# PSUM operands, GpSimd minima and a shorter backward scan in the WKV ratio of a fused two-layer kernel

## The chip, the cores and the metric

The kernel runs on one core of one Trainium2 chip, as one launch. The metric is the device time of the whole program in microseconds. A core has five engines that each run their own instruction queue: PE (TensorE, matmuls), DVE (VectorE), ACT (ScalarE), POOL (GpSimd) and SP (SyncE, which here issues the DMAs). On-chip memory is SBUF (128 partitions) and PSUM (128 partitions, here used as banks of 128x512 float32; matmuls write to it). All data is float32.

## The reference

Four sequences of 256 tokens with 256 channels pass two layers. Each layer is: condition the activations, mix the tokens, add; condition again, a feed-forward net with experts, add. In layer 0 the mixing is a gated delta-rule attention, and the net has 64 experts; in layer 1 the mixing is a gated linear block, and the net has 8 experts. What the change touches above all is the conditioner, which occurs four times, with its own `w` and `u` (k and v are both the side input f, r is the activation):

```python
def _bi_wkv(r, k, v, w, u, time_emb):
    tf = sigmoid(sum(time_emb, axis=-1))[:, None, None]
    decay = exp(-exp(w))[None, :] * (0.5 + 0.5 * tf[:, :, 0])
    ek = exp(minimum(kf, 30.0))
    ekv = ek * vf
    # step: a = a * decay + ekv_t ; b = b * decay + ek_t, kept after every token
    _, (nf, df) = scan(step, 0, (ekv_t, ek_t))
    _, (nb, db) = scan(step, 0, (ekv_t, ek_t), reverse=True)
    euk = exp(minimum(u + kf, 30.0))
    num = nf + nb - ekv + euk * vf
    den = df + db - ek + euk
    base = sigmoid(r) * (num / maximum(den, 1e-08))
    return base * (0.8 + 0.2 * tf)
```

Everything but `sigmoid(r)` depends on the inputs alone, so `num / den` (the ratio) of all four conditioners can be made at any time before it is needed.

The attention of layer 0, per head and chunk of 64 tokens:

```python
g = cumsum(-exp(a_log) * softplus(x @ w_a + dt_bias))       # log decay in the chunk
q, k, v = split(silu(conv4(x @ w_qkv)))                     # q and k are then l2-normed
A = where(strict, -(beta * k @ k.T) * exp(g_i - g_j), 0)
attn = solve_triangular(I - A, I)                           # a 64x64 unit triangular inverse
v_c, k_c = attn @ (v * beta), attn @ (k * beta * exp(g))
# then a scan over the chunks with a 128x128 state per head
out = rmsnorm(o) * norm_w * silu(x @ w_z) @ w_out
```

## The kernel before

**Tape and plan.** The program isn't issued as it is written. Every piece of work is recorded with `Tape.op` (line 195): its engine, an assumed cost in us, the function that emits its instructions, the buffers it reads and writes, and, for ACT, the function table that it needs. [...] `pushed` (391) works new latest starts out of a finished plan, and `run` (405) plans again with them, up to `ROUNDS` times. Of these plans it takes the one with the lowest end (`min(plans)`, line 413), and emits all operations in the order of their starts. Each engine keeps the emitted order (`Ordered`, 118). So the instruction order of every engine, and the order in which buffers go round, come out of the plan, and any changed cost or constant (lines 421 to 428) may change the order anywhere in the program. All recorded instructions carry line 128 in the profile; they are told apart by the names of their tiles.

**Buffers.** `ps` (1474) hands out six PSUM banks that all uses share: convolutions (`ps_cvq`, `ps_cvk`, `ps_cvv`), Gram matrices (`ps_gram`), norms (`ps_kt`), 32- and 64-wide products of the inverse (`ps_at` and others, `ps_lu`), `ps_z`, `ps_wo`, the experts (`ps_h`, `ps_a`, `ps_e`, `ps_ae`). `place` (1464) hands out 59 SBUF tiles of 128x512, and the table `MOST` says how many of these each use may hold at a time.

**Stages.** Tokens go in two halves of 512, s = 0 and 1.

1. Conditioner 0 of half 0 (`conditioned`, `ratio_piece` with c = 0), then `gates` (1679): `ps_gates`, the decay `g` by several small DVE and ACT operations, `ps_decay`, a row form written to DRAM (`G<-rows`), which is read back spread over partitions (`attnT<-G`, per head).
2. Attention in four groups of four key heads per half (`Group`, with a `Unit` per key head that has two value heads). `Unit.products` (882): convolutions with four taps (`convolved`; PE, then three SCALAR_TENSOR_TENSOR on DVE and one ACT activation), Gram matrices, norms (`norms`, `shifted`: squares are summed on PE into a `kt` bank, transposed by DVE into an SBUF tile `turned`, and made into reciprocal norms), the decay masks (`attnT`: DVE or ACT adds, ACT exp, POOL products with `sb_consts`, with `c` and with the Gram matrices `kqm`, which make `X`). `Group.small_inverses` (493): X goes to DRAM (`raw<-X`) and comes back in a layout with one 32x32 problem to a partition (`Rt<-raw`); DVE solves it there by 30 pairs of operations (`prod`, `xs`), transposes it (`Tc`), and DMAs it back through DRAM (`done`). `inverse32` and `inverse64` make the 64x64 inverses with matmuls (`ps_lu` and what follows). Then `values`, `outputs`, `normed`, `project` (`ps_wo`).
3. The 64 experts (`experts64`; weights `w_w` come by DMA for each expert pair), conditioner 2 of layer 1's `gated_mix`, and the 8 experts (`experts8`), each for both halves.

**The ratio** (`ratio_piece`, 1521): a conditioner c has eight pieces, one for each channel half cc and sequence b, each of 128 channels x 256 tokens; 32 in all. The four pieces with c = 0 and s = 0 are "summed": their three terms of `num` and of `den` are added by PE, with an identity matrix, in a PSUM bank. In the other 28, POOL adds them in SBUF, and with c > 0 the result waits in DRAM until its layer needs it. In a piece, DVE makes the two minima, ACT the two exponentials `ek` and `euk`, POOL `ekv`, `euk - ek` and the product with f (into f); DVE makes four scans over 256 tokens (`fwn`, `bwn`, `fwd`, `bwd`), each with the decay of the channel, then the maximum, the reciprocal and the product with the numerator. Both scans include a token itself, which is why `ek` is subtracted once (`num` needs no such operation, as `(euk - ek) * f` has it).

Of the kernel before, what the change touches and what calls it, by code (L numbers as in the profile page):

```python
# [11 lines left out]
AF = mybir.ActivationFunctionType  # L12
ALU = mybir.AluOpType
# [3 lines left out]
P = 128  # L17
# [164 lines left out]
class Tape:  # L182
# [222 lines left out]
    def run(self):  # L405
        latest, plans = self.urgency(), []
        for n in range(ROUNDS):
            last = self.plan(latest)
            if last is None:
                break  # L410
            plans.append((last, n, [(o.start, o.end, o.new) for o in self.ops]))
            latest = self.pushed(last)
        for o, (o.start, o.end, o.new) in zip(self.ops, min(plans)[2]):
            pass
        for o in sorted(self.ops, key=lambda o: (o.start, o.order)):
            for buf in o.new:
                buf()
            o.emit()


ROUNDS, SWITCH, LOAD, SPARE, AHEAD, EACH, END, IDLE, MOMENT, GAP, RATE, GIVES = 10, 14.532, 1.3, 95.787, 163.973, 23.222, 1300.0, 54.829, 0.668, 62.664, 3.14, 4.877
UNIT = 42

EARLY, FEW = range(3, 5), 6
NORMS = 0.55
FOUR32, TWO64 = 0.75, 1.1
LAND = 3.0
WINDOW, ENOUGH, LITTLE, SLOW, THIN = 3.4, 0.471, 0.38, 0.5, 6.598
# [367 lines left out]
class Unit:  # L796
# [85 lines left out]
    def products(self):  # L882
# [65 lines left out]
        turned = self.buf([P, 8, 32], "turned", 2)  # L948
        sums = lambda j: turned().rearrange("p (n j) r -> p n j r", j=2)[:, :, j, 0]
# [28 lines left out]

        op("PE", NORMS, norms, sqs, [ps], to=[turned, k2, ki, self.kn, self.eo])

# [398 lines left out]
class Program:  # L1379
# [82 lines left out]
    MOST = {'attnT': 20, 'kq1': 12, 'kq0': 2, 'kqm': 17, 'cross': 10, 'vo': 18, 'zs': 5, 'oT': 6, 'w0': 5, 'hw0': 9, 'w1': 8, 'hw1': 7, 'wo': 2, 'sq': 4, 'r0': 10, 'wqk': 20, 'vn': 21, 'acck': 22, 'wb0': 3, 'vd': 7, 'U': 5, 'wv': 7, 'qe': 6}  # L1462
# [58 lines left out]
    def ratio_piece(self, c, cc, b):  # L1521
# [28 lines left out]
        op(  # L1550
            "DVE",
            0.45,
            lambda: v.tensor_scalar(
                euk(), f(), self.wu[:, c, 1, cc : cc + 1], 30.0, ALU.add, ALU.min
            ),
# [5 lines left out]
        op("POOL", 0.75, lambda: tt(ekv(), ek(), f(), ALU.mult), [ek, f], [ekv])  # L1561
        op("POOL", 0.75, lambda: tt(euk(), euk(), ek(), ALU.subtract), [ek], [euk])
        op("POOL", 0.75, lambda: tt(f(), euk(), f(), ALU.mult), [euk], [f])
        decay = self.decay[:, c, cc, b : b + 1].to_broadcast([P, T])

        def sums(n, *terms):

            to = ps()[:, n * T : n * T + T]
            for i, x in enumerate(terms):
                last = i == len(terms) - 1  # L1570
                e.tensor.matmul(to, self.const(IDENT), x(), start=i == 0, stop=last)

        def both_ways(src, extra, n):
            fw, bw = new(f"fw{n}"), new(f"bw{n}", f"bw{n}" if summed else "bw")
            op(
                "DVE",
                0.95,
                lambda: v.tensor_tensor_scan(fw(), decay, src(), 0.0, ALU.mult, ALU.add),
                [src, self.decayb],
                [fw],  # L1580
            )
            op(
                "DVE",
                0.95,
                lambda: v.tensor_tensor_scan(
                    bw()[:, ::-1], decay, src()[:, ::-1], 0.0, ALU.mult, ALU.add
                ),
                [src, self.decayb],
                [bw],
            )  # L1590
            if summed:
                i = "nd".index(n)
                op(
                    "PE",
                    _mm(256, 3),
                    lambda: sums(i, fw, bw, extra),
                    [fw, bw, extra],
                    [(ps, {i})],
                )
                return lambda: ps()[:, i * T : i * T + T], (ps, {i})  # L1600
            op("POOL", 0.75, lambda: tt(fw(), fw(), bw(), ALU.add), [bw], [fw])
# [3 lines left out]
        num, numb = both_ways(ekv, f, "n")  # L1605
        sum_, sumb = both_ways(ek, euk, "d")
        den = new("den") if summed else sumb
        op("DVE", 0.45, lambda: v.tensor_scalar_max(den(), sum_(), 1e-8), [sumb], [den], port=True)
        op("DVE", 1.75, lambda: v.reciprocal(den(), den()), [], [den])
# [4 lines left out]
        else:  # L1614
# [7 lines left out]
            [numb, den, self.decayb],  # L1622
            [w],
            port=True,
# [632 lines left out]
```

## Time and profile before

| what | value |
| --- | --- |
| time, median of 3 runs | 1410.57 us (1408.24 to 1412.5) |
| the profiled execution: time, span | 1412.93 us, 1411.1 us |
| mean granted PE clock | 0.982 of full speed |
| PE busy | 1321.2 us, 94% of the span |
| DVE busy | 1064.8 us, 75% |
| POOL busy | 922.8 us, 65% |
| ACT busy | 915.2 us, 65% |
| ACT table loads | 126, 161.7 us |
| chain of waits that ended last, by engine | PE 45%, DVE 25%, ACT 12%, POOL 7%, DMA 6% |
| start of the first 64-wide products (`ps_lu`) of the eight groups | 152, 244, 353, 470, 579, 695, 805, 901 us |

The mean durations of one instruction of a ratio piece (the 26 or 28 that are not among the first), all 128x256:

| engine | instruction | mean ns |
| --- | --- | --- |
| DVE | minimum into `ek`, sum and minimum into `euk` | 491, 562 |
| DVE | scans `fwd`, `bwd`, `fwn`, `bwn` | 913, 837, 881, 1016 |
| DVE | maximum, reciprocal, product with the numerator | 486, 1748, 612 |
| POOL | `ekv`, `euk - ek`, product with f | 730, 823, 782 |
| POOL | the four additions | 728, 956, 767, 748 |

How to read it: "busy" is the time in which an engine worked on an instruction of its own; register and semaphore instructions do not count. A matmul's end is modelled, so a busy PE need not be PE at its peak. The span is one profiled execution from its first to its last instruction; the time of that execution is 1.8 us longer. Where the text below gives a moment, it is a start in us from the start of the span. The engines overlap nearly everywhere, so busy times do not add up to the span.

### The profile page before, as it was taken

Reading aid. Unit: us, or ns where it says so; the run is one execution under the profiler, and the core shown is the slowest. Engines: PE = TensorE matmul, PEld = TensorE weight load, DVE = VectorE, ACT = ScalarE, POOL = GpSimd, SP = SyncE. Lnnn points to the kernel's source line nnn. Section 1 sums busy time; section 2 is a strip of 40 time slices with the busy share of each in tenths; the row PEclk is TensorE's granted clock in tenths of the full one; section 3 lists DMA queues with packets and bytes.
Section 4 is the critical chain, followed back from the end, with each engine's and each line's share of the span. In section 5 each row is a group of like instructions: output and inputs, shape, how many; then the busy total and the mean of one; then the engine's idle time right before and its main releaser. Section 6 shows DMA issues by size and latency. Waiting matters only on the chain.

```text
span 1411.1 us, 24205 instructions
## 1 busy us (share of the span) xinstructions
PE 1321.2 (94%) x8428; PEld 817.4 (58%) x8428; DVE 1064.8 (75%) x2112; ACT 915.2 (65%) x1999; POOL 922.8 (65%) x913
## 2 busy tenths in 40 slices
PE   5986999999999899999999999999999999998988
PEld 3544766765875676766676576555455544443433
DVE  7889798787699588768769879867796787773123
ACT  1797799999889899988898898533434622211220
POOL 3189769979763988976885884487654666762032
PEclk9997999999999999999999999999999999999989
DMA  6412524412322353241351343544532324656030
GB/s 208 129 46 64 128 83 113 125 62 67 91 90 58 71 140 106 50 139 39 94 139 38 76 124 101 150 127 135 153 105 83 103 92 139 181 139 212 0 105 15
DMA packets 149817, 145.39 MB, mean 103 GB/s; under 512 B 76976, under 2 KB 93104, under 8 KB 149696
## 3 DMA queue, kind: packets, MB, share of 16 engines
q1 hardware_dynamic: 149264, 143.45, 35.5%
q8 instruction: 67, 1.10, 0.3%
q14 instruction: 54, 0.44, 0.1%
q10 hardware_dynamic: 432, 0.40, 0.1%
HBM read 129.75 MB, written 14.06 MB: 102 GB/s over the span
## 4 chain that ended last, share of the span: by engine, by line
PE 45%; DVE 25%; ACT 12%; POOL 7%; DMA 6%; issue 5%; SPq 1%; ACTq 0%; POOLq 0%; DVEq 0%
PE ps_h L128 5%; PE ps_a L128 4%; PE ps_ae L128 4%; PE ps_wo L128 4%; PE ps_e L128 4%; PE ps_z L128 4%; DVE xs L128 3%; DVE prod L128 3%; DVE accv_v L128 3%; PE ps_cvv L128 3%; PE ps_at L128 2%; DVE accq_q L128 2%; POOL attnT L128 2%; DMA w_w<-in_w 2%; ACT L128 2%
## 5 line engine op out<-in xcount | busy, mean ns | idle before, releaser
L128 ACT ACT_TABLE_LOAD x126 | 161.7, 1283 | 22.2 <-DVE sb_xT L128 10.4
L128 DVE SCALAR_TENSOR_TENSOR accv_v<-ps_cvv,sb_convw,accv_v 128x510 f32<-128x510 f32 (+2 forms) x192 | 141.8, 744 | 42.3 <-ACT accv_v L128 37.4
L128 PE MATMUL ps_z<-wz,ratio 128*128 128x256 f32 x480 | 118.7, 394 | 9.6 <-DVE vo L128 6.6
L128 POOL TENSOR_TENSOR hw_h<-hw_h,r_h 128x512 f32<-128x512 f32 x64 | 85.7, 1347 | 63.9 <-DVE hw_h L128 63.3
L128 PE MATMUL ps_h<-ratio,w_w 128*128 128x512 f32 x256 | 118.9, 598 | 6.6 <-DMA w_w<-in_w 5.7
L128 PE MATMUL ps_cvv<-ratio,wv 128*128 128x512 f32 x256 | 119.9, 601 | 2.9 <-ACT kqm L128 1.0
L128 ACT ACTIVATE r_h<-ps_h 128x512 f32<-128x512 f32 x64 | 38.2, 596 | 126.8 <-PE ps_h L128 126.5
L128 PE MATMUL ps_a<-hw_h,w_w 128*128 128x512 f32 x256 | 118.2, 593 | 0.0
L128 PE MATMUL ps_wo<-oT,wo 128*128 128x512 f32 x256 | 113.0, 593 | 0.0
L128 POOL TENSOR_TENSOR hw_e<-hw_e,r_e 128x512 f32<-128x512 f32 x32 | 41.6, 1322 | 101.0 <-DVE hw_e L128 101.0
L128 PEld LDWEIGHTS ps_z<-wz,ratio 128*128 128x128 f32 x480 | 90.1, 196 | 24.6 <-DVE vo L128 6.8
L128 PEld LDWEIGHTS ps_h<-ratio,w_w 128*128 128x128 f32 x256 | 47.0, 190 | 70.2 <-issue 55.1
L128 DVE TENSOR_TENSOR xs<-xs,prod 128x30 f32<-128x30 f32 (+14 forms) x240 | 81.2, 338 | 8.2
L128 DVE TENSOR_TENSOR prod<-xs,Rt 128x30 f32<-128x30 f32 (+14 forms) x240 | 78.5, 327 | 11.6 <-ACT xs L128 5.9
L128 ACT ACTIVATE junko<-vo 128x128 f32<-128x128 f32 x256 | 79.3, 310 | 7.6
L128 PE MATMUL ps_at<-vn,attnT 128*128 128x128 f32 x512 | 82.3, 277 | 1.5 <-ACT vn L128 1.4
L128 POOL TENSOR_TENSOR X<-attnT,kqm 128x512 f32<-128x512 f32 x64 | 82.8, 1313 | 1.2 <-ACT kqm L128 1.0
L128 POOL TENSOR_TENSOR vo<-vo,zs 128x512 f32<-128x512 f32 x64 | 81.2, 1288 | 1.6 <-ACT zs L128 1.6
L128 PEld LDWEIGHTS ps_wo<-oT,wo 128*128 128x128 f32 x256 | 48.1, 190 | 57.4 <-issue 52.6
L128 POOL TENSOR_TENSOR attnT<-attnT,sb_consts 128x512 f32<-128x512 f32 x56 | 70.7, 1280 | 15.5 <-DMA attnT<-G 8.5
L128 POOL TENSOR_TENSOR attnT<-attnT,kqm 128x512 f32<-128x512 f32 x64 | 80.6, 1278 | 0.1
L128 PEld LDWEIGHTS ps_a<-hw_h,w_w 128*128 128x128 f32 x256 | 47.9, 190 | 56.2 <-issue 52.6
(253 smaller groups left out, 3412.5 us busy)
## 6 DMA issues: line engine op xcount, KB each, us to landing
attnT<-G SPq DMA_DIRECT2D x64, 256.0 KB, 5.2
w_w<-in_w SPq DMA_DIRECT2D x64, 256.0 KB, 4.4
wb_wb<-w_rows SPq DMA_DIRECT2D x128, 128.0 KB, 3.6
wqk<-in_wqk SPq DMA_DIRECT2D x32, 256.0 KB, 4.2
wv<-in_wv SPq DMA_DIRECT2D x32, 256.0 KB, 4.2
wo<-in_wo SPq DMA_DIRECT2D x32, 256.0 KB, 3.8
qe<-G SPq DMA_DIRECT2D x32, 256.0 KB, 4.5
wz<-in_wz SPq DMA_DIRECT2D x30, 256.0 KB, 4.6
```

The lines of the kernel that those rows point to most:

```text
L128: return self._tc.keep_in_program_order(f(*a, **k))
```

## The change

- **Exponentials in PSUM.** `ek` is written by ACT into the left half of a PSUM bank `both`, of which each piece takes one. `ekv = ek * f` is made by DVE into its right half (before: by POOL, in SBUF). All four scans read their terms from there, and write to SBUF as before.
- **The backward scan without the own token.** It runs over 255 tokens, adds first and multiplies after: `b_t = (b_(t+1) + x_(t+1)) * decay`. With that `- ek` and `- ekv` fall away: POOL's `euk - ek` is gone, and the product of `euk` and f goes to `low` (the tile of the first minimum) and no more over f. The sum of the two scans has 255 columns.
- **Minima.** In the 28 unsummed pieces both run on POOL (assumed cost `MINS` = 0.6), in the four summed ones on DVE as before.
- **Maximum and reciprocal.** In the unsummed pieces they write to and read from a PSUM bank `den` (before: in place in SBUF); the last product reads it there.
- **Fewer, larger records.** The product and the two scans of the numerator are one recorded operation (DVE, 1.8), the two scans of the denominator another (1.4), the maximum and the reciprocal a third (2.2). What is in one record can't be parted by other work.
- **Norms.** `shifted` transposes the norms into the right half of their own `kt` bank, and reads them there; the SBUF tile `turned` is gone. Its assumed cost is 0.92 in place of 0.78.
- **The plan.** `ROUNDS` is 4 in place of 10, and `run` takes the last plan in place of the one with the lowest end. Several constants of the planner and several entries of `MOST` (`vo` 18 to 15, `r0` 10 to 3, `acck` 22 to 18, `w1` 8 to 6, `w0` 5 to 6, `U` 5 to 2, and others) differ.

```diff
-        for o, (o.start, o.end, o.new) in zip(self.ops, min(plans)[2]):
+        for o, (o.start, o.end, o.new) in zip(self.ops, plans[-1][2]):
...
-ROUNDS, SWITCH, LOAD, SPARE, AHEAD, EACH, END, IDLE, MOMENT, GAP, RATE, GIVES = 10, 14.532, 1.3, 95.787, 163.973, 23.222, 1300.0, 54.829, 0.668, 62.664, 3.14, 4.877
-UNIT = 42
+ROUNDS, SWITCH, LOAD, SPARE, AHEAD, EACH, END, IDLE, MOMENT, GAP, RATE, GIVES = 4, 11.718, 1.3, 106.8, 160.0, 23.99, 1300.0, 54.95, 0.68, 66.3, 3.14, 5.0
+UNIT = 42.358
...
-NORMS = 0.55
-FOUR32, TWO64 = 0.75, 1.1
+NORMS = 0.6
+FOUR32, TWO64 = 0.72, 1.1
+MINS = 0.6
...
-WINDOW, ENOUGH, LITTLE, SLOW, THIN = 3.4, 0.471, 0.38, 0.5, 6.598
+WINDOW, ENOUGH, LITTLE, SLOW, THIN = 3.4, 0.42, 0.38, 0.5, 10.339
...
-        turned = self.buf([P, 8, 32], "turned", 2)
-        sums = lambda j: turned().rearrange("p (n j) r -> p n j r", j=2)[:, :, j, 0]
+        turned = lambda: ps()[:, 256:]
+        sums = lambda j: turned().rearrange("p (n j r) -> p n j r", j=2, r=32)[:, :, j, 0]
...
-            v.transpose(turned().rearrange("p x t -> p (x t)"), ps()[:, :256])
+            v.transpose(turned(), ps()[:, :256])
...
-        op("DVE", 0.78, shifted, [ps], [turned, k2, ki, self.eo])
+        op("DVE", 0.92, shifted, [], [ps, k2, ki, self.eo])
...
-        ek, ekv, euk = new("ek"), new("ekv"), new("euk")
+        both, low, euk = self.ps(f"both{c}{cc}{b}"), new("ek"), new("euk")
+        ek, ekv = (lambda: both()[:, :T]), (lambda: both()[:, T:])
         v, tt, act = e.vector, e.gpsimd.tensor_tensor, e.scalar.activation
-        op("DVE", 0.45, lambda: v.tensor_scalar_min(ek(), f(), 30.0), [f], [ek], port=True)
-        op("ACT", 0.4, lambda: act(ek(), ek(), AF.Exp), [], [ek], table="exp")
...
+        ts = (v if summed else e.gpsimd).tensor_scalar
+        few, cost = ("DVE", 0.4) if summed else ("POOL", MINS)
+        op(few, cost, lambda: ts(low(), f(), 30.0, None, ALU.min), [f], [low], port=True)
         op(
-            "DVE",
-            0.45,
...
+            few,
+            cost,
+            lambda: ts(euk(), f(), self.wu[:, c, 1, cc : cc + 1], 30.0, ALU.add, ALU.min),
             [f],
             [euk],
             port=True,
         )
         op("ACT", 0.4, lambda: act(euk(), euk(), AF.Exp), [], [euk], table="exp")
-        op("POOL", 0.75, lambda: tt(ekv(), ek(), f(), ALU.mult), [ek, f], [ekv])
-        op("POOL", 0.75, lambda: tt(euk(), euk(), ek(), ALU.subtract), [ek], [euk])
-        op("POOL", 0.75, lambda: tt(f(), euk(), f(), ALU.mult), [euk], [f])
+        op("ACT", 0.4, lambda: act(ek(), low(), AF.Exp), [low], [both], table="exp")
+        op("POOL", 0.75, lambda: tt(low(), euk(), f(), ALU.mult), [euk, f], [low])
...
+            def scans():
+                if n == "n":
+                    v.tensor_tensor(ekv(), ek(), f(), ALU.mult)
+                v.tensor_tensor_scan(fw(), decay, src(), 0.0, ALU.mult, ALU.add)
+                v.tensor_tensor_scan(
+                    bw()[:, T - 2 :: -1],
+                    src()[:, T - 1 : 0 : -1],
+                    decay[:, : T - 1],
+                    0.0,
+                    ALU.add,
+                    ALU.mult,
+                )
+
+            if n == "n":
+                op("DVE", 1.8, scans, [f, self.decayb], [both, fw, bw])
+            else:
+                op("DVE", 1.4, scans, [both, self.decayb], [fw, bw])
+            earlier = lambda: bw()[:, : T - 1]
...
-            op("POOL", 0.75, lambda: tt(fw(), fw(), bw(), ALU.add), [bw], [fw])
+            to = lambda: fw()[:, : T - 1]
+            op("POOL", 0.75, lambda: tt(to(), to(), earlier(), ALU.add), [bw], [fw])
             op("POOL", 0.75, lambda: tt(fw(), fw(), extra(), ALU.add), [extra], [fw])
             return fw, fw
...
-        den = new("den") if summed else sumb
-        op("DVE", 0.45, lambda: v.tensor_scalar_max(den(), sum_(), 1e-8), [sumb], [den], port=True)
-        op("DVE", 1.75, lambda: v.reciprocal(den(), den()), [], [den])
+        if summed:
+            den = denb = new("den")
+        else:
+            bank = self.ps(f"den{c}{cc}{b}")
+            den, denb = (lambda: bank()[:, :T]), bank
+
+        def inverted():
+            v.tensor_scalar_max(den(), sum_(), 1e-8)
+            v.reciprocal(den(), den())
+
+        op("DVE", 2.2, inverted, [sumb], [denb])
...
-            [numb, den, self.decayb],
+            [numb, denb, self.decayb],
             [w],
-            port=True,
         )
```

More of the change, by code (lines that the diff above doesn't have):

```diff
@@ L977, in norms @@
                     )
-        op("PE", NORMS, norms, sqs, [ps], to=[turned, k2, ki, self.kn, self.eo])
+        op("PE", NORMS, norms, sqs, [ps], to=[k2, ki, self.kn, self.eo])
         tt = e.gpsimd.tensor_tensor
@@ L1460 @@
     PLACES = 59
-    MOST = {'attnT': 20, 'kq1': 12, 'kq0': 2, 'kqm': 17, 'cross': 10, 'vo': 18, 'zs': 5, 'oT': 6, 'w0': 5, 'hw0': 9, 'w1': 8, 'hw1': 7, 'wo': 2, 'sq': 4, 'r0': 10, 'wqk': 20, 'vn': 21, 'acck': 22, 'wb0': 3, 'vd': 7, 'U': 5, 'wv': 7, 'qe': 6}
+    MOST = {'attnT': 20, 'kq1': 12, 'kq0': 2, 'kqm': 18, 'cross': 11, 'vo': 15, 'zs': 6, 'oT': 6, 'w0': 6, 'hw0': 8, 'w1': 6, 'hw1': 8, 'wo': 2, 'sq': 4, 'r0': 3, 'wqk': 20, 'vn': 21, 'acck': 18, 'wb0': 3, 'U': 2}
     def place(self, use, name, shape=(P, 512)):
@@ L1545, in ratio_piece @@
         ps = self.ps(f"ratio{cc}{b}") if summed else None
-        ek, ekv, euk = new("ek"), new("ekv"), new("euk")
+        both, low, euk = self.ps(f"both{c}{cc}{b}"), new("ek"), new("euk")
+        ek, ekv = (lambda: both()[:, :T]), (lambda: both()[:, T:])
         v, tt, act = e.vector, e.gpsimd.tensor_tensor, e.scalar.activation
-        op("DVE", 0.45, lambda: v.tensor_scalar_min(ek(), f(), 30.0), [f], [ek], port=True)
-        op("ACT", 0.4, lambda: act(ek(), ek(), AF.Exp), [], [ek], table="exp")
-        op(
-            "DVE",
-            0.45,
-            lambda: v.tensor_scalar(
-                euk(), f(), self.wu[:, c, 1, cc : cc + 1], 30.0, ALU.add, ALU.min
-            ),
+        ts = (v if summed else e.gpsimd).tensor_scalar
+        few, cost = ("DVE", 0.4) if summed else ("POOL", MINS)
+        op(few, cost, lambda: ts(low(), f(), 30.0, None, ALU.min), [f], [low], port=True)
+        op(
+            few,
+            cost,
+            lambda: ts(euk(), f(), self.wu[:, c, 1, cc : cc + 1], 30.0, ALU.add, ALU.min),
             [f],
@@ L1560, in ratio_piece @@
         op("ACT", 0.4, lambda: act(euk(), euk(), AF.Exp), [], [euk], table="exp")
-        op("POOL", 0.75, lambda: tt(ekv(), ek(), f(), ALU.mult), [ek, f], [ekv])
-        op("POOL", 0.75, lambda: tt(euk(), euk(), ek(), ALU.subtract), [ek], [euk])
-        op("POOL", 0.75, lambda: tt(f(), euk(), f(), ALU.mult), [euk], [f])
+        op("ACT", 0.4, lambda: act(ek(), low(), AF.Exp), [low], [both], table="exp")
+        op("POOL", 0.75, lambda: tt(low(), euk(), f(), ALU.mult), [euk, f], [low])
         decay = self.decay[:, c, cc, b : b + 1].to_broadcast([P, T])
         def sums(n, *terms):
-            to = ps()[:, n * T : n * T + T]
             for i, x in enumerate(terms):
+                at = x()
+                to = ps()[:, n * T : n * T + at.shape[1]]
                 last = i == len(terms) - 1
-                e.tensor.matmul(to, self.const(IDENT), x(), start=i == 0, stop=last)
+                e.tensor.matmul(to, self.const(IDENT), at, start=i == 0, stop=last)
         def both_ways(src, extra, n):
             fw, bw = new(f"fw{n}"), new(f"bw{n}", f"bw{n}" if summed else "bw")
[L1575 to L1590, printed above, removed]
+            def scans():
[15 more added lines that the diff above has]
+            earlier = lambda: bw()[:, : T - 1]
             if summed:
@@ L1594, in both_ways @@
                     "PE",
-                    _mm(256, 3),
-                    lambda: sums(i, fw, bw, extra),
+                    1.73,
+                    lambda: sums(i, fw, earlier, extra),
                     [fw, bw, extra],
@@ L1600, in both_ways @@
                 return lambda: ps()[:, i * T : i * T + T], (ps, {i})
-            op("POOL", 0.75, lambda: tt(fw(), fw(), bw(), ALU.add), [bw], [fw])
+            to = lambda: fw()[:, : T - 1]
+            op("POOL", 0.75, lambda: tt(to(), to(), earlier(), ALU.add), [bw], [fw])
             op("POOL", 0.75, lambda: tt(fw(), fw(), extra(), ALU.add), [extra], [fw])
             return fw, fw
-        num, numb = both_ways(ekv, f, "n")
+        num, numb = both_ways(ekv, low, "n")
         sum_, sumb = both_ways(ek, euk, "d")
-        den = new("den") if summed else sumb
-        op("DVE", 0.45, lambda: v.tensor_scalar_max(den(), sum_(), 1e-8), [sumb], [den], port=True)
-        op("DVE", 1.75, lambda: v.reciprocal(den(), den()), [], [den])
+        if summed:
[7 more added lines that the diff above has]
+        op("DVE", 2.2, inverted, [sumb], [denb])
         part = {(cc, b % 2)}
```

## The prediction

> **What bounds the kernel now.** I read the busy slices first, then TensorE's (PE's) work by stage, then what ended its idle time, then the timeline of the stretch with the worst idle time.
>
> The busy slices: each digit is the busy share of a fortieth of the span in tenths.
>
> ```profile
> PE   5986999999999899999999999999999999998988
> ...
> DVE  7889798787699588768769879867796787773123
> ...
> PEclk9997999999999999999999999999999999999989
> ```
>
> PE is full but for slices 1, 3, 4, 14 and the last four; in slice 4 (105 to 141 us) its clock falls too. PE by stage (stretch, length, PE busy, granted clock, DMA share, GB/s):
>
> ```profile
> 35.00:70.00 35.00, 31.89 (x143) 0.94 0.43 123
> 70.00:105.00 35.00, 28.92 (x112) 0.95 0.20 53
> 105.00:140.00 35.00, 21.07 (x103) 0.78 0.18 61
> ...
> 175.00:455.00 280.00, 273.04 (x2135) 1.00 0.30 84
> 455.00:490.00 35.00, 28.98 (x387) 0.95 0.35 93
> 490.00:1190.00 700.00, 684.02 (x4501) 1.00 0.37 105
> 1190.00:1330.00 140.00, 133.31 (x307) 1.00 0.50 149
> 1330.00:1411.00 81.00, 69.88 (x165) 0.92 0.15 52
> ```
>
> PE works 1321.2 of 1411.1 us. Of the 90 idle us, some 17 precede the first gates, 23 lie in 35 to 140, 6 at 455 to 490, 23 in the two long full stretches (7 + 16), 7 late, 11 in the tail. Only these can be won, and only new idle time on PE can be lost: PE's instructions are the same 4480 in both programs. PE's waits (us in total, times, longest):
>
> ```profile
> PE ps_kt L128 <- ACT kqm L128: 7.1, 2, 6.1
> PE ps_z L128 <- DVE vo L128: 6.6, 1, 6.6
> PE ps_h L128 <- DMA w_w<-in_w: 5.7, 10, 1.3
> ```
>
> The first two lie at 118 and 136 us: PE has run out of work while the first group's inverse is made. That chain is, in the timeline (start, length, engine, operation):
>
> ```profile
> 49.33 0.29 DVE L128 TENSOR_TENSOR g<-sp_ekv,na 128x128 f32<-128x128 f32 x1
> ...
> 111.01 0.18 DVE L128 TENSOR_TENSOR prod<-xs,Rt 128x30 f32<-128x30 f32 x1
> ...
> 135.14 0.20 DVE L128 TENSOR_TENSOR xs<-xs,prod 128x30 f32<-128x30 f32 x1
> ...
> 52.79 0.33 SPq L128 DMA_DIRECT2D G<-rows  x1
> ...
> 97.76 2.69 POOL L128 TENSOR_TENSOR X<-attnT,kqm 128x512 f32<-128x512 f32 x2
> ...
> 100.48 2.59 SPq L128 DMA_DIRECT2D raw<-X  x4
> ```
>
> So: decay g 49.6, G written 52.8 and spread, X masked and multiplied on POOL until 100.5, written and read back turned (raw, Rt), xs solved on DVE 111 to 135, and then PE's 32-wide products (142.6) and 64-wide ones (152.4).
>
> **The ratio's pieces.** There are 32, four of them summed on PE. Two rows of DVE, beside other work and alone:
>
> ```profile
> 7.75 0.68 DVE L128 TENSOR_TENSOR_SCAN first_fwd_fwd<-decay,first_ek_ek 128x256 f32<-128x256 f32 x1
> 8.35 1.14 DVE L128 TENSOR_TENSOR_SCAN first_bwd_bwd<-decay,first_ek_ek 128x256 f32<-128x256 f32 x1
> ```
>
> The second runs while POOL is at its own two-input operations. Scans of the later pieces average 0.84 to 1.02 (0.91). If the PSUM source ends this slowing, a scan costs 0.68; if not, 0.91. DVE per unsummed piece: two minima go (0.49 + 0.56), a product comes (0.42, as the 256-wide PSUM maximum of the first pieces), four scans gain 4 x 0 to 4 x 0.23: 0.6 to 1.5 us, times 28 is 18 to 43 us. POOL: two operations go (0.82 + 0.73), two minima come. A minimum on POOL is not in the trace; bounds are DVE's uncontended 0.28 and POOL's two-input 0.82; I take 0.6, nearer its own engine. Per piece -1.0 to +0.1, taken -0.35, times 28 is -10 us. I count both at nothing: DVE has 25% and POOL 35% free, and PE's full stretches cover them. Without that cover, at the ratio pieces that PE waits for, a piece is worth at most its 1.5 us.
>
> [...]
>
> **The opening.** Here the order matters more than the prices, so I compared the two programs' instruction orders, engine by engine, and added durations of the rows above.
> - First ratio: ten scans of 1.14 become 0.68 (-4.6), four products come (+1.7); against that two of the minima now stand late in DVE's queue, and ACT changes its table (1.28 each way) from exp to sigmoid and back before the last exps. I get 32.4 instead of 31.8 us: +0.6 (-3 to +2).
> - g: the old order has three groups of convolution taps (three operations, 2.3 us a group) ahead of g on DVE, the new one seven, a 0.68 copy and two turns of norms (0.9 each): 4 x 2.3 + 0.7 + 1.8 = 11.7 later. On PE 13 convolutions stand ahead of ps_decay instead of 8, and the last needs an eighth tap group to free its bank. So the G write goes out at about 65.9, not 52.8 (+13.1).
> - X: behind G's landing POOL has 35 us of work until group 0's last X, against 24.6 before, but with fewer waits (it took 32 us of wall then), so X ends at 111.5 (+11).
> - xs: raw to xs takes 10.5 us as before, xs starts at 122 (+11). Seven us of other DVE work are interleaved with the 23 to 24 of the solve: 30 us in place of 24.4. The 32-wide products start at 158.6 (+16).
> - PE meanwhile has more to do: ahead of those products stand 97.8 us of matmuls instead of 86.1 (+11.7), so 4 to 5 us are lost there. Between them and the 64-wide ones stand 3.2 us of matmuls instead of 8.8: those start at 166 (+13.6) with 6.1 us more done.
> New idle time by then: 13.6 - 6.1, about **+8**. Low end: if the uncontended scans and free POOL bring X 10 us sooner, xs falls back to PE's own work: -2. High end: the six units' later work does not fill up what I took as filled: +14.
>
> **PSUM banks.** Each piece now holds one of the six banks from exp to scans (and `den` one again): over the 32 pieces, from the orders, 659 + 161 us of PE work, so 820 of 6 x 1321, or 0.62 of a bank always gone. The 23 us of idle time in the full stretches are mostly short waits for evictions; with 5.38 banks for 6 they grow by 11%: 2.6, taken **+3** (0 to +10: the top adds the longest bank wait that was seen, 7). Keeping the turned norms in their bank holds it 0.5 us longer, 32 times: 16 us more, nothing; uncovered, at most 0.5 us once in each group's norms.
>
> [...]
>
> **Second half and late.** At 454 us the DMA that returns group 3's inverse stood behind the burst of attnT<-G of the second half and took 8.1 us; that window idles 6. The new order issues it ahead of the burst: **-3** (-6 to +3, since the burst then hits something else). The last ratio piece now stands at 1114 us of PE's work, not 1198, out of the way of the second experts: part of 7 idle us, **-2** (-7 to +4; fewer buffers, 6 for 8, for the weights whose DMA already cost 5.7). Tail: same order, **0**.
>
> **Sum.** +8 + 3 - 3 - 2 = +6. The profiled execution took 1412.93 (span 1411.1 and 1.8 around it), which gives 1419; it lies 2.4 above the median 1410.57, and a run of after should compare with that: **1417**.
>
> **Rivals.**
> - *The relief wins* (30%): the opening's lateness is covered by the extra 11.7 us of convolutions and faster scans (-2), banks cost 0 to 1, s=1's bubble goes (-5) and the late scans too (-3): 1402. For: DVE works 25% of the chain of waits. Against: nearly all of that is convolution taps and xs, not scans.
> - *Banks bind* (18%): a `both` bank waits for its scans from 40 to 99 us and again at 395 to 470 and 565 to 635 of PE's work. If PE is held by the fifth bank for each convolution in these stretches, 205 us at 5% idle more, +10, on top of +8: 1429. It decides from 2% more idle time on. Against: the rows of the middle have little waiting.
> - *Nothing moves* (12%): opening +4, banks +1, gains -5: 1411. Also the case in which the new order is just another of equal worth.
> - The change not doing what it says: scans that are as slow from PSUM as before; my sum gives them nothing, so it stays.
>
> **How the numbers follow.** A measurement of this kernel tells 0.3% (4.2 us) from no change. My case (40%) holds 1409 to 1425; six of its 40 parts end within 0.3%. Slower: 34 + 18 = 52%; same 6 + 12 = 18%; faster 30%. The range takes in both: 1399 to 1434.
>
> **What would show it.** G written near 66 and xs from about 122 us; 105 to 140 us fuller and 140 to 175 emptier; scans at 0.68 with DVE down by 18 to 43 us; the window at 455 fuller; PE idle shares in the middle up by under 1%. If G goes out before 58, the opening term falls; if PE's waits name `both`'s readers, the bank rival holds.

## The result, and the profile after

| | before | after |
| --- | --- | --- |
| median of 4 runs, us | 1411.11 (1408.24 to 1412.5) | 1423.41 (1422.09 to 1425.54) |
| ratio to before, 95% interval | 1 | 1.0095 [1.0077, 1.0114] |
| profiled execution, span, us | 1411.1 | 1421.2 |
| mean granted PE clock | 0.982 | 0.972 |
| busy us: PE, DVE, POOL, ACT | 1321.2, 1064.8, 922.8, 915.2 | 1327.7, 1011.8, 898.1, 912.0 |

The changed kernel is slower by 0.95%; the medians lie 12.3 us apart, the two profiled executions 10.1. DVE works 53 us less, POOL 25 less, and PE, with the same matmuls, 6.5 us more. The page of after, busy time and the slices (tenths, 40 to the span):

```profile
PE 1327.7 (93%) x8428; PEld 826.8 (58%) x8428; DVE 1011.8 (71%) x2088; ACT 912.0 (64%) x1999; POOL 898.1 (63%) x905
...
PE   4958799999999999999999999899999999999988
...
PEclk8999799999999999999999999899999999999989
```

The weak slices are still at the front (1, 3, 4, 5), and in 1 and 5 the clock dips too; the one at 14 is gone, and a new one, with a dip of the clock, stands at 26. PE by stage in after (stretch, length, PE busy, granted clock, DMA share, GB/s):

```profile
35.00:70.00 35.00, 32.67 (x113) 0.90 0.01 3
70.00:105.00 35.00, 20.75 (x83) 0.90 0.47 154
105.00:140.00 35.00, 29.16 (x173) 0.93 0.22 54
140.00:175.00 35.00, 24.52 (x297) 0.74 0.41 91
...
455.00:490.00 35.00, 32.75 (x358) 1.00 0.49 123
875.00:910.00 35.00, 28.76 (x436) 0.85 0.30 70
1190.00:1330.00 140.00, 137.02 (x322) 1.00 0.55 156
1330.00:1411.00 81.00, 75.34 (x178) 0.94 0.16 52
```

and, in the same view of before, the two stretches that were not shown:

```profile
140.00:175.00 35.00, 32.20 (x521) 0.97 0.57 132
...
875.00:910.00 35.00, 32.64 (x309) 1.00 0.42 111
```

The idle time has moved from 105 to 140 us (21.1 busy before, 29.2 now) to 70 to 105 (28.9, now 20.8) and 140 to 175 (32.2, now 24.5). The bubble at 455 has closed (29.0, now 32.8), and one has opened at 875. The clock column holds what the sum did not: 0.74 in 140 to 175, and 0.85 at 875. The same columns for the stretches in which the clock record of after stands at one half:

```profile
18.80:29.04 10.24, 7.00 (x16) 0.50 0.87 334
35.87:42.69 6.82, 6.82 (x16) 0.51 0.01 1
...
148.51:155.33 6.82, 5.94 (x19) 0.51 0.39 129
165.57:182.64 17.07, 12.25 (x300) 0.50 0.66 126
896.02:906.26 10.24, 7.70 (x163) 0.50 0.25 39
```

The first ratio's sums, for instance, start 0.85 us apart at half clock and 0.43 at full; so each such stretch is counted as half of PE's busy time in it lost, an estimate from these two. All of them make 80.2 us in after (30.4 us of PE work lost) and 52.8 in before (18.7 lost).

To see where the time was lost, I took milestones (the starts of certain matmuls) and subtracted from each how much PE work, at full clock, stands ahead of it in that program's own order, so that work which only changed places drops out. What is left is the loss up to there, idle time and half clock together; after minus before, from the two profiled executions:

| milestone | start before, after (us) | loss, after minus before |
| --- | --- | --- |
| `ps_gates` | 31.3, 34.5 | +3.2 |
| first 32-wide products | 142.6, 162.5 | +8.2 |
| first 64-wide products | 152.4, 171.8 | +13.3 |
| first `ps_wo` | 193.0, 214.0 | +16.5 |
| `ps_gates` of the second half | 421.4, 413.2 | +16.3 |
| first `ps_wo` of the second half | 522.5, 534.2 | +9.0 |
| `ps_wo` of its last group | 846.6, 861.1 | +9.4 |
| first expert | 884.4, 902.7 | +14.8 |
| layer 1's `ps_in` of the second half | 1302.5, 1312.9 | +10.4 |
| end of the span | 1411.1, 1421.2 | +10.1 |

So the opening cost 16.5, the second half's start gave back 7.3, the end of the attention cost 5.4 and the late part gave back 4.7. The opening's 16.5 divides into about 9 of PE at half clock (up to the first `ps_wo` such stretches lose 10.4 us of work in before and 19.7 in after) and about 7 of idle time.

PE's longest waits in after (us in total, times, longest):

```profile
PE ps_lx L128 <- DMA X<-done: 8.5, 4, 5.3
PE ps_gram L128 <- DVE kqm L128: 7.9, 1, 7.9
PE ps_ratio L128 <- DVE first_fwn_fwn L128: 7.8, 1, 7.8
```

The waits of 7.1 and 6.6 us, at 118 and 136 us in before, are gone. The first row now is the return of the inverse through DRAM, the second the idle time ahead of a Gram matrix at 97.7, the third the kernel's very start, ahead of the first sums.

The scans did become faster. Groups of after (busy us, mean ns, idle just before):

```profile
L128 POOL TENSOR_SCALAR euk<-f,sb_wu 128x256 f32<-128x256 f32 x26 | 30.4, 1168 | 5.2 <-DVE sp_ekv L128 2.6
L128 POOL TENSOR_SCALAR ek<-f 128x256 f32<-128x256 f32 x26 | 22.3, 858 | 3.1 <-DVE acck_k L128 0.9
...
L128 DVE TENSOR_TENSOR_SCAN fwn<-decay,ps_both 128x256 f32<-128x256 f32 x26 | 17.8, 686 | 6.7 <-DMA ratios<-fwn 5.9
...
L128 DVE TENSOR_TENSOR_SCAN bwd<-ps_both,decay 128x255 f32<-128x255 f32 x26 | 17.3, 664 | 8.6 <-POOL fwn L128 8.6
...
L128 DVE TENSOR_SCALAR k<-ps_kt 128x4 f32<-128x4 f32 x32 | 5.2, 161 | 1.3
```

and of before:

```profile
L128 DVE TENSOR_SCALAR k<-turned 128x4 f32<-128x4 f32 x32 | 12.7, 396 | 1.5
```

All four scans lie between 662 and 686 ns, where before they took 837 to 1016. A norm's tiny sum of 4 columns fell from 396 to 161 ns with PSUM as its source.

### The profile page after: what moved, and what is told of

It is laid out like the page before. It is cut to its first block, busy times and chain, and to the rows that moved or that the text cites. A ratio compares the mean times of both kernels' runs of the same rounds, so it can differ in the third digit from the quotient of the medians.

```text
span 1421.2 us, 24241 instructions
## 1 busy us (share of the span) xinstructions
PE 1327.7 (93%) x8428; PEld 826.8 (58%) x8428; DVE 1011.8 (71%) x2088; ACT 912.0 (64%) x1999; POOL 898.1 (63%) x905
## 4 chain that ended last, share of the span: by engine, by line
PE 44%; DVE 21%; POOL 12%; ACT 8%; DMA 6%; issue 5%; SPq 1%; POOLq 0%; ACTq 0%; DVEq 0%
PE ps_h L128 5%; PE ps_a L128 5%; PE ps_wo L128 5%; PE ps_ae L128 4%; POOL attnT L128 4%; PE ps_cvv L128 4%; PE ps_e L128 3%; DVE xs L128 3%; DVE prod L128 3%; DVE accq_q L128 3%; PE ps_z L128 3%; DVE acck_k L128 2%; PE ps_gram L128 2%; POOL X L128 2%; DVE accv_v L128 2%
## 5 line engine op out<-in xcount | busy, mean ns | idle before, releaser
L128 POOL TENSOR_TENSOR hw_h<-hw_h,r_h 128x512 f32<-128x512 f32 x64 | 80.9, 1268 | 79.8 <-DVE hw_h L128 75.7
L128 PE MATMUL ps_z<-wz,ratio 128*128 128x256 f32 x480 | 115.3, 388 | 1.3 <-PE ps_z L128 0.6
L128 DVE SCALAR_TENSOR_TENSOR hw_h<-ps_h,wb_wb 128x512 f32<-128x512 f32 x64 | 44.1, 689 | 64.5 <-ACT r_h L128 51.4
L128 POOL TENSOR_TENSOR vd<-vn,dc 128x512 f32<-128x512 f32 x32 | 33.3, 1040 | 87.1 <-ACT vn L128 87.0
```

Source lines behind the costliest of these rows:

```text
L128: return self._tc.keep_in_program_order(f(*a, **k))
```

## Experiments

A ratio is to before, with its 95% interval; before was measured again beside each group of runs, with medians of 1407.4 to 1411.3 us. In comparisons with after, after is the 1.0095 above; 0.001 is 1.4 us. "First `ps_wo`" is 214.0 us in after, 193.0 in before.

### The parts in a plan of their own

The four runs of this section exchange operations under new plans or under the other program's order. `e2_old_ops` has after's planner constants and before's `ratio_piece` and `shifted`; `e3_new_ops` has before's constants and ten plans, with after's operations:

```diff
 # e2, in before; e3, in after, has the same lines the other way round
-        for o, (o.start, o.end, o.new) in zip(self.ops, min(plans)[2]):
+        for o, (o.start, o.end, o.new) in zip(self.ops, plans[-1][2]):
...
-UNIT = 42
+UNIT = 42.358
...                     # the other constants and MOST likewise
```

> The changed planner constants with the ratio's and the norms' old operations. Theory A (the loss comes from the order that the new plan gives the opening: g and what hangs on it late, PE idle, and PE's clock halved after it; the new operations themselves cost PE nothing): in this kernel's order six tap groups stand ahead of g and 101 us of matmuls ahead of the first 32-wide products, so it opens late too, at 1416 to 1424 us. Theory B (the new operations cost it: PSUM banks held, slower minima on POOL): without them 1411 us or less.

> The new operations with the old planner constants (ten plans, the one that ends first). Its order has four tap groups ahead of g and 82 us of matmuls ahead of the first 32-wide products. Theory A: G is written near 55 us, and the time is 1400 to 1412 us. Theory B: 1418 us or more, with PE waiting for banks in the middle.

1466.2 us, 1.0385 [1.035, 1.0421], and 1466.18 us, 1.0384 [1.0355, 1.0414]. Both combinations lose 55 us against before. For e2 no theory foresaw it; for e3 it lies above the open bound of theory B, but those of PE's waits in e3 that name a reader of the new banks come to 5.6 us. In both runs constants and operations that were not chosen for each other cost 55 us, so a part of this change can't be priced by planning it anew, and in all further runs the order was held.

`e10_new_ops_old_order` issues after's operations in before's order, `e11_old_ops_new_order` the reverse; where a record has no counterpart it stands at its nearest one, and buffers are handed out again along the order. `e19_own_order` is the control: after's own order through the same code.

```diff
-        for o in sorted(self.ops, key=lambda o: (o.start, o.order)):
+        starts = ...          # the positions in the other program's order
+        for o in self.replay(starts):   # first in that order whose inputs and buffer are there
```

> The new operations, emitted in the order of the kernel before (each new operation at the place of the old one it stands for; one that finds no free bank is put off until there is one). Theory A (the order is what costs): 1403 to 1414 us, G written near 53 us, the first 32-wide products near 143. Theory B (the new operations cost, through banks held and slow minima on POOL): 1418 us or more.

> The other way round: the old operations of the ratio and the norms, emitted in the order of the changed kernel. Theory A: as slow as the changed kernel or slower by what the old operations cost DVE and POOL, 1420 to 1432 us. Theory B: 1415 us or less.

> A control: the changed kernel emitted by the same replay of a fixed order as the runs with swapped orders, but in its own order. All theories: within 3 us of the changed kernel. If it is 10 us or more slower, the replay itself (where buffers are taken) costs, and the runs with swapped orders say less.

| run | us | ratio | first `ps_wo` |
| --- | --- | --- | --- |
| e10 | 1455.81 | 1.0339 [1.0308, 1.0371] | 205.9 |
| e11 | 1480.24 | 1.0509 [1.0473, 1.0545] | 227.1 |
| e19 | 1422.73 | 1.0094 [1.0076, 1.0112] | 216.3 |

The control sits on after, so replaying costs nothing that shows in the time, and 3.4% and 5.1% are what the operations cost in an order made for others. e11 lies far above both of its forecasts, e10 in the open range of its theory B. PE's waits in e10 (total us, times, longest) show one place:

```profile
PE ps_ratio L128 <- DVE first_fwd_fwd L128: 18.8, 4, 10.9
```

The numerator's record, with the product in it, has to stand ahead of the denominator's scans, and PE's sums wait, 10.3 us longer than in before (8.5). That is not all: e10's span is 42.3 us longer than before's, and 12.9 of these are lost by the first `ps_wo`; what costs the rest was not followed up. So e10 misfits and does not price the operations alone.

### One operation at a time, in a held order

`e8_minima_dve` takes after and its order, with all minima on DVE. `e9_scan_sbuf` does the same with `ek` and `ekv` in SBUF (two tiles in turn); the bank stays reserved and unused, so the plan is the same.

```diff
-        ts = (v if summed else e.gpsimd).tensor_scalar
+        ts = v.tensor_scalar                                    # e8
...
-        ek, ekv = (lambda: both()[:, :T]), (lambda: both()[:, T:])
+        ek, ekv = (lambda: sb()[:, :T]), (lambda: sb()[:, T:])  # e9
```

> The changed kernel in its own order, all minima on DVE. POOL took 0.86 and 1.17 us for one, where my prediction took 0.6; on DVE they should take 0.3 to 0.5. If POOL's price costs time, 2 to 6 us less than the changed kernel; if PE covers it, within 2 us of it.

> The changed kernel in its own order, with the exponential and its product with f kept in SBUF (the bank stays reserved and unused). If the PSUM operand is what makes the scans fast, they go from 0.67 back to 0.8 to 1.0 us and POOL's operations beside them get slower; on the time that is worth 0 to 4 us where PE covers DVE, more if it doesn't. If the shorter scan is what makes them fast, the forward scans stay at 0.67.

e8: 1427.38 us, 1.0138 [1.0111, 1.0166], 4 to 6 us above after, with DVE at 1031.8 and POOL at 841.3; neither outcome that was expected. e9: 1443.16 us, 1.025 [1.022, 1.028], 20 to 22 us above after. Two scans of e9, and its busy times:

```profile
L128 DVE TENSOR_TENSOR_SCAN bwd<-sb,decay 128x255 f32<-128x255 f32 x26 | 27.9, 1075 | 9.4 <-POOL fwn L128 9.4
...
L128 DVE TENSOR_TENSOR_SCAN fwn<-decay,sb 128x256 f32<-128x256 f32 x26 | 24.8, 955 | 4.5 <-DMA ratios<-fwn 3.7
```

```profile
PE 1336.4 (93%) x8428; PEld 832.1 (58%) x8428; DVE 1053.7 (73%) x2088; ACT 914.0 (63%) x1999; POOL 917.1 (64%) x905
```

The same scans over 255 or 256 columns take 0.80 to 1.08 us from SBUF and 0.66 to 0.69 from PSUM: DVE gains 42 us by it and POOL 19. And this DVE time is not covered by PE: handed back in a fixed order it costs 20 us, with DVE 27% idle. (The two tiles in turn show no cost of their own: ACT's idle time ahead of writing them is put down to POOL's minima, 31.2 of 32.3 us, and never to a scan that still reads them.)

`e17_no_banks` is e10 with exponential, product and denominator in SBUF, and no bank reserved: after's operations, SBUF operands, before's order.

> The new operations in the order of the kernel before once more, but with exponential, product and denominator in SBUF, so that no bank is taken. If it was the banks that made the same thing with banks 45 us slower than before, this is 1400 to 1416 us, with the first gates near 31 to 33. If it was the minima on POOL or the records that were joined, 1430 us or more.

1443.21 us, 1.0235 [1.0214, 1.0256], 13 to 15 us under e10: there the banks (which in that order no plan had made room for) cost more than the faster scans give. The 33 us that e17 still loses against before fall to the other side of its expectation: minima on POOL, joined records or slower scans in an order not made for them. No run parts these; PE's longest wait is the same as in e10 (`ps_ratio` on `first_fwd_fwd`, 19.4 us in total).

`e13_short_scan` is before with its own order, and nothing but the backward scan without its own token; POOL's subtraction keeps its place in the plan and emits nothing.

```diff
-        op("POOL", 0.75, lambda: tt(euk(), euk(), ek(), ALU.subtract), [ek], [euk])
+        op("POOL", 0.75, lambda: None, [ek], [euk])
```

> The kernel before in its own order, with one part of the change alone: the backward scan leaves out its own token, and POOL's 32 subtractions fall away (0.82 to 0.96 us each, 27 us of POOL in all). If POOL's time is covered, 1408 to 1412 us; if freed POOL time shortens the ratio's and the masks' chains in this order, 1400 to 1407.

1412.72 us, 1.0019 [1.0003, 1.0035]: POOL works 27 us less, and the median gains nothing. In the profiled execution the first `ps_wo` comes 4.4 us sooner. One of PE's waits in it:

```profile
PE ps_h L128 <- DMA w_w<-in_w: 9.4, 11, 2.8
```

In before that wait was 5.7 in total, so 3.7 us more go into waiting for the experts' weights. But the profiled execution is the fastest of the ten (1409.68 us), and its span still ends 3.2 us ahead of before's; where the 4.4 us go in the median is not shown.

### The late minima

In after's opening (start, length, engine, operation, idle time and what ended it):

```profile
23.27 0.60 DVE L128 TENSOR_SCALAR first_euk_euk<-first_f_f,sb_wu 128x256 f32<-128x256 f32 x2
23.64 0.72 ACT L128 ACTIVATE first_euk_euk<-first_euk_euk 128x256 f32<-128x256 f32 x2 [10.18 <-DVE first_euk_euk L128]
...
24.14 1.41 POOL L128 TENSOR_TENSOR first_ek_ek<-first_euk_euk,first_f_f 128x256 f32<-128x256 f32 x2 [9.87 <-ACT first_euk_euk L128]
...
27.93 0.42 DVE L128 TENSOR_SCALAR first_den_den<-ps_ratio 128x256 f32<-128x256 f32 x1 [3.99 <-PE ps_ratio L128]
```

The two minima of 0.30 us each stand behind all scans; ACT and POOL stood idle for ten us before them, and DVE then waits four for PE's sums. `e5_minima_early` moves these two, their exponentials and their products to 10.6 to 13.4 us of the plan, ahead of the scans.

```diff
+        for i, at in (42, 10.62), (54, 10.92), (43, 12.61), (55, 12.62), (45, 13.41), (57, 13.42):
+            self.ops[i].start = at
```

> The changed kernel in its own order, but the two late minima of the first ratio (with their exponentials and products) are put right behind the first minima. The first gates start near 30 to 31 us instead of 34.5. If what is lost there stays lost, 2 to 5 us less than the changed kernel; if a later wait takes it up, no change.

1418.92 us, 1.0062 [1.0039, 1.0086], 4.5 us under after. DVE's timeline in e5 at the same point:

```profile
22.65 0.78 DVE L128 SCALAR_TENSOR_TENSOR ratio<-ps_ratio,tfo,first_den_den 128x256 f32<-128x256 f32 x2
23.34 0.14 DVE L128 TENSOR_SCALAR sb_normw<-sb_normw 128x1 f32<-128x1 f32 x1
23.47 0.42 DVE L128 TENSOR_SCALAR first_den_den<-ps_ratio 128x256 f32<-128x256 f32 x1
```

The wait of 3.99 is gone, the gates come at 29.5 for 34.5, and the first `ps_wo` at 209.9. Part of that wait was PE's clock, since the sums ahead of it lie in the stretch at half clock from 18.80 on: in e7 (next section), where the minima are as late but PE is kept busy (granted clock 1.00 in 0 to 35 us), DVE waits 2.21 us there, and the gates start at 32.4.

### PE's clock

`e7_busy` keeps PE busy in after at seven idle places (five in the opening, two at 893 to 900) with 82 extra 128x128 matmuls, whose result is overwritten; `e14_dense` adds 40 among the small products of the first group; `e20_between` is e5 in whose order 6.9 us of full matmuls that are needed anyway are put among those small products; `e21_before_busy` is before with 50 extra matmuls, ahead of the first gates, of a Gram matrix and of the late router.

```diff
+        warm = {37: 12, 49: 12, 68: 12, 628: 10, 313: 20, 3265: 7, 3272: 9}    # e7
+        warm |= {422: 8, 320: 8, 427: 8, 323: 8, 434: 8}                       # e14 too
+        warm = {88: 30, 232: 12, 4861: 8}                                      # e21
...
+            for _ in range(warm.get(o.order, 0)):
+                self.warm(bank())       # identity x identity into o's own bank, ahead of o
             o.emit()
```

> The changed kernel in its own order, with 82 dummy 128x128 matmuls put into seven places where PE idles (into a bank that is overwritten afterwards). If idle time is what halves PE's clock a moment later, the half-clock stretches at 19 to 29, 36 to 43, 148 to 155, 166 to 183 and 896 to 906 us shrink or vanish and the time falls by 4 to 10 us, to 1413 to 1419. If the clock follows something else (load, the kind of matmul), the stretches stay where they are, and the time is that of the changed kernel or up to 2 us more, 1423 to 1426.

> The changed kernel with the dummy matmuls in the idle places as before, and 40 more between the 32- and 64-wide products at 165 to 183 us. If PE's clock is halved because these small products use little of the array (there was no idle time ahead of the half-clock stretch at 167 to 184 when only the idle places were filled), that stretch vanishes, and the time is 2 to 5 us below the run with idle places filled; if not, the stretch stays and the time is up to 6 us above it.

> The changed kernel with the two late minima early, and four blocks of full-width matmuls that stand some 20 us later in its order (three convolutions with their taps, one block for the gate z, 6.9 us of PE work) put between the first group's 32- and 64-wide products. If the string of small products is what keeps PE at half clock for 20 us there, that stretch falls under 8 us and the time by 3 to 6 us against the run with the minima alone, to 1413 to 1416 us. If the group's own chain decides there, no gain or a loss: 1418 to 1424 us.

> The kernel before with 50 dummy matmuls in three of its idle places (ahead of the first gates, of a Gram matrix at 74 us, and of the router's logits at 1337 us). If idle time halves the clock here too, the half-clock stretches at 29 to 39, 74 to 77 and 1340 to 1347 us shrink, and the time falls by 2 to 5 us, to 1405 to 1408 us; if not, it stays within 2 us.

| run | us | ratio | half clock, us (work lost) | first `ps_wo` |
| --- | --- | --- | --- | --- |
| before | | 1 | 52.8 (18.7) | 193.0 |
| after | 1423.41 | 1.0095 [1.0077, 1.0114] | 80.2 (30.4) | 214.0 |
| e7 | 1420.27 | 1.0058 [1.0032, 1.0084] | 59.2 (22.5) | 211.7 |
| e14 | 1425.22 | 1.0113 [1.0086, 1.0141] | 43.0 (16.0) | 216.6 |
| e20 | 1423.91 | 1.0114 [1.0092, 1.0137] | 73.1 (26.9) | 219.2 |
| e21 | 1403.71 | 0.9968 [0.9952, 0.9984] | 26.4 (8.4) | 188.5 |

With work placed in idle time less of the span stands at half clock (59.2 for 80.2 us in e7, 26.4 for 52.8 in e21), and the gain is 3 to 5 us in after (e7, whose interval touches after's) and 4 in before (e21, which beats both kernels). It gains less than the 8 to 10 us of work that the clock gives back; that DVE, POOL and DMA set the pace in part of the opening would explain it, and no run shows it. The clock's share can't be read off as time: e14 has less half clock than before itself, and is no faster than after. The longest stretch did not go in e7 (same columns as above):

```profile
166.93:183.99 17.06, 16.33 (x221) 0.51 0.32 82
```

PE is busy through it, and the clock is still one half; 9.1 of the 16.3 busy us are 32- and 64-wide products, the rest 128-wide. It was not free of idle time ahead, as the expectation of e14 has it: of the 3.4 us just before it PE idled 1.6. e14 cuts the stretch to 3.4 us and takes 5 to 8 us more time than e7. e20 has 10.24 us there in place of e5's 20.48, and a new stretch of 6.83 behind; the products come later, and it takes 5 to 7 us more than e5. That stretch could be shortened and nothing was won.

### The chain to the first inverse, sooner

`e4_g_early` puts `g` and all that depends on it 12 us earlier in after's order, within the first 135 us. `e15_chain12`, `e16_chain18` and `e18_chain24` take e5 and move all that the first 32-wide products wait for by 12, 18 and 24 us (replayed as e19; 156 records change place against after).

```diff
+    def moved(self, by=12.0, until=135.0):          # e4; e15, e16, e18: their ancestors, 12, 18, 24
+        ...
+            if o.start < until:
+                o.start = max([o.start - by] + [self.ops[i].start + 1e-3 for i in o.before])
```

> The changed kernel in its own order, but g and everything that hangs on it within the first 135 us of the plan stand 12 us further ahead in their queues. Theory A: G is written near 56 us, the first 32-wide products start near 150, less PE time at half clock, 1410 to 1415 us. Theory B: the lateness is covered elsewhere and it stays at 1421 us or more.

> The changed kernel with the two late minima early, and everything that the first 32-wide products wait for (g, the norms, Gram matrices, masks, X, its way through DRAM, the solve) up to 12 us further ahead in every queue; 88.6 us of matmuls are left ahead of these products in place of 97.8. If the opening's order is what costs, 1412 to 1417 us; if the opening is covered by what comes later, 1419 or more.

> The same with up to 18 us: four tap groups ahead of g instead of seven, 86.1 us of matmuls ahead of the first 32-wide products, as in the kernel before. If the opening's order is what costs, 1408 to 1414 us, G written near 56 and the first 32-wide products before 150; if not, 1419 or more.

> The same with up to 24 us: 79.1 us of matmuls ahead of the first 32-wide products. If earlier is better without limit, below the run with 18 us; if PE runs out of work ahead of the products, 2 to 8 us above it.

| run | us | ratio | G written | `raw<-X` | first `ps_wo` |
| --- | --- | --- | --- | --- | --- |
| after | 1423.41 | 1.0095 [1.0077, 1.0114] | 67.7 | 115.6 | 214.0 |
| e4 | 1452.12 | 1.0289 [1.0248, 1.0329] | 55.8 | 126.3 | 242.7 |
| e15 | 1443.23 | 1.0242 [1.0221, 1.0263] | 61.7 | 123.2 | 236.3 |
| e16 | 1447.43 | 1.0278 [1.0259, 1.0296] | 58.7 | 120.2 | 236.6 |
| e18 | 1444.93 | 1.0258 [1.0242, 1.0275] | 55.6 | 119.1 | 238.2 |

G did come 12 us sooner in e4, and X still 11 later. PE's waits in e4, and in e16:

```profile
PE ps_gram L128 <- DVE prod L128: 12.8, 1, 12.8
PE ps_kt L128 <- ACT sq L128: 9.3, 2, 6.4
```

```profile
PE ps_kt L128 <- ACT sq L128: 15.1, 3, 12.1
```

What is moved up seems to wait at the head of its queue for what was not, and to block what stands behind it. In all four PE waits longer for ACT's squares (`sq`): 9.3, 7.3, 15.1 and 16.3 us in e4, e15, e16 and e18, against 3.0 in after. So whether a better order of the opening exists with these operations is not settled by them. Beside the other runs in after's order they show how far lateness at the first `ps_wo` arrives at the end:

| against after | e5 | e7 | e14 | e20 | e19 | e15 | e16 | e18 | e4 |
| --- | --- | --- | --- | --- | --- | --- | --- | --- | --- |
| first `ps_wo`, us | -4.1 | -2.3 | +2.6 | +5.2 | +2.3 | +22.3 | +22.6 | +24.2 | +28.7 |
| median, us | -4.5 | -3.1 | +1.8 | +0.5 | -0.7 | +19.8 | +24.0 | +21.5 | +28.7 |

The first row comes from one execution each, and the control e19 (+2.3 and -0.7) shows how much of it can be chance. The 20 to 29 us of the last four arrive; for the small ones the rows don't decide, and e20 is an exception.

## Why the prediction was right or wrong

It foresaw slower, by 6 us, with the opening's new order as the cause. It is slower by 12, and the largest loss does arise in the opening; that its order is the cause follows from the milestones, while the runs that moved the chain forward (e4, e15, e16, e18) gave nothing back. The terms:

- **The opening (+8): wrong in size, +13.3 at the 64-wide products and +16.5 at the first `ps_wo`.** The moments were near: G 67.7 (said 65.9), `raw` 115.6 (111.5), `xs` 126.9 (122), the first 32-wide products 162.5 (158.6), the 64-wide ones 171.8 (166). The step that failed is "New idle time by then: 13.6 - 6.1". It counted idle time alone, and up to the first `ps_wo` that came out at about 7; but it priced PE's work at full clock, and PE lost another 9 at half clock. The row was at hand: 0.78 in 105 to 140 us of before.
- **"+0.6 (-3 to +2)" for the first ratio: +3.2**, beyond its bound. The two late minima were seen and priced as two instructions. The price is the chain behind them: ACT, POOL, PE at half clock, and four us of DVE waiting. e5 gets 4.5 us back from them. (Of the scans ahead of before's first gates eight, not ten, took 1.14 to 1.18 us; the others took 0.66 to 0.83.)
- **The banks (+3): +0.4** between the second half's first `ps_wo` and the last group's. Among PE's waits in after a reader of `both` is named twice, for 2.1 us in all, and the norms' reader of their bank (`eo`) three times, for 4.3; the longer of the first two is `PE ps_ot <- DVE bwd`, 1.8 us at 1133. That is the sign which the prediction gave for the bank rival, at a size far below the rival's 10 us; no run in after's order gives the banks back. In before's order banks did cost (e10 against e17, 13 us).
- **Second half's start (-3): -7.3**, past its low bound of -6. The mechanism held: the return of the inverse stands ahead of the burst now, and takes 2.6 us (issued at 452.8, `X<-done` at 455.4) in place of 8.1. **Late (-2): -4.4**, in its bounds; **tail (0): -0.3**.
- **Not in the sum:** +5.4 at the end of the attention (861 to 903 us), where PE waits for `X<-done` and the clock halves (0.50 from 896.02 to 906.26). No run parted the two, and e7, which took most of that half clock, touched the opening too.
- **Luck.** The opening and the end of the attention came out 14 us above the sum, banks, second half, late part and tail 10 us below it. So the total is nearer than its terms.
- **The relief counted at nothing since "PE's full stretches cover them": not so in after's order.** DVE got 53 us (said 18 to 43: the norms' small sums, counted at nothing, gave 15 more). e9 shows that in after's order some 42 of DVE and 19 of POOL are worth 20 us. In before's order 27 us less on POOL are worth nothing (e13). So these orders lost by what was lengthened (e8, e9) and did not gain by what was shortened (e13); that it is so for other orders is not shown. In its own order the changed kernel needs its faster scans.
- **A minimum on POOL, 0.6 us (0.28 to 0.82): 0.86 and 1.17**, both above the upper bound. That bound was POOL's two-input row of 0.82; its other two-input rows in before reach 0.96. On DVE the same two took 0.49 and 0.56 in before, beside other work. The kernel is no slower for it: in e8, with the minima on DVE, it takes 4 to 6 us more.

Of the rivals, nothing moving fell by the time, and banks binding by the trace (+0.4). The relief is real and did not win, since the opening's lateness was not covered. Settled by runs: 4.5 us from the late minima, 3 to 5 from filling idle time, and that a lateness of 20 us in the opening passes through. The first two overlap: both bring the first gates sooner, e7 by 2.0 of e5's 5.0 us. So some 5 to 7 of the 12 us stay without an experiment that returns them, and their cause stays argued.

## What to carry to other kernels

When a change moves idle time about on PE, read the granted clock beside the busy time, stretch by stretch: here the time at half clock rose from 52.8 to 80.2 us, which a sum of idle time leaves out. Filling idle places with matmuls whose result is not used brought the old kernel's 52.8 us down to 26.4 (e21) and made it faster by 0.32%. An instruction that has become late is priced by what stands idle behind it on the other engines, not by its own length. And here a plan that was tuned for one set of operations did not price another: hold the order, change one operation in it, and run a control of the held order.

## What the runs showed of the hardware

In the clock record of before and after every stretch stands at full or at one half, and each that lies at one half with matmuls in it lasts 3.41, 6.83, 10.24 or 17.07 us. PE's timeline of after at the start of the stretch of 148.51:

```profile
149.39 0.65 PE L128 MATMUL ps_kt<-sq,ones 128*32 128x128 f32 x8 [2.98 <-ACT sq L128]
```

Of this idle time of 2.98 us, 2.1 lie ahead of the stretch, which has 6.8 us at half clock; in before an idle time of 2.1 us at 665 stands ahead of 3.4 us at half clock. Of the 19 gaps of 1.3 to 1.9 us in the two traces 15 have no half clock within the next 3.4 us. Of the 18 stretches at half clock in before and after that have matmuls in them, 17 follow on 3.41 us in which PE was busy for 0 to 1.64 us, and one, at 489.7 in after, on 2.04 (0.97 of it 32- and 64-wide products). How much idle time halves the clock, and whether small products weigh in, these counts do not settle.

With their terms in PSUM the scans also lost nothing beside POOL. Scans with both operands in SBUF that overlap a POOL operation took 0.98 us on average in before and 1.14 in e9, and those that overlap none took 0.68 and 0.67; with the terms in PSUM (after) they took 0.67 either way. The two kinds of minimum on POOL differ by more than a third, 0.86 us with one operation and 1.17 with two.
